# A copy of q placed above the relative terms in SBUF, and a pair of low-rank products split in two

## The chip, the cores and the metric

The kernel runs on one NeuronCore of a Trainium2 chip. The metric is the device time of one execution in microseconds (us). Before the change three runs gave a median of 3314.61 us (3313.37 to 3317.38).

## The reference

Two attention layers work on one image of 48 x 48 positions with 768 channels. Each adds its result to its input:

```python
x = x + L0(_gn(x))          # plus low-rank terms on q and v
x = x + L1(_gn(x))

# inside a layer, per head (12 heads of 64):
qkv  = x @ qkv_w + qkv_b
attn = einsum('bqc,bkc->bqk', q * scale, k)
rel_h = einsum('bhwc,hkc->bhwk', r_q, Rh)      # by the query's row
rel_w = einsum('bhwc,wkc->bhwk', r_q, Rw)      # by the query's column
attn = softmax(attn + rel_h[..., :, None] + rel_w[..., None, :])
out  = (attn @ v) @ proj_w + proj_b
```

`_gn` is a group norm over 32 groups of 24 channels. In layer 0 a product of rank 16 (`FacTu_w`, `q_facts_w`, `v_facts_w`, `FacTv_w`) is added to q and v; the kernel folds it into the weights.

## The kernel before

All data is 32-bit. Channels lie on partitions. The 2304 positions are cut into six blocks of 384 for the projections (`b`), and into four blocks of 512 and one of 256 for attention's queries. Twelve heads are six pairs, and a "half" is three pairs.

A layer runs in this order.

1. **Norm** (`group_norm`, from L194). Channel means and variances are summed over groups by small matmuls (`sum_mean`, then `sum_var`) and spread back over channels by others (`bc_mean`, then `bc_rstd`). The order of PE's instructions is held by `in_order`. While one step waits for DVE, PE is given other work: `next(between)` resumes the generator `low_rank` (L313 to L339), which in layer 0 forms the low-rank products `psl` (L336) and copies them to SBUF (`low`, L339). In its loop over two halves each resume issues two products. In layer 1 there is no low-rank term and the generator is empty.
2. **k and v** (`project_kv`). Results are stored to scratch memory in HBM. The last tile of values, `v_2_2`, is stored by 16 DMAs of GpSimd's queue (L599).
3. **q** (`project_q`, from L601). For each half, six blocks are multiplied (L695) and biased (L701), stored as two parts, high and low (`store`, L628), and copied by ACT to the tile `columns` with rows and columns of the image exchanged (L711). PE then forms `rel_h` from each block (L635, stored at L661). When the half is complete, `rel_w` is formed from `columns` (L635 again, sixteen steps), split into a high part by ACT (L389) and a low part by DVE (L390), and stored by two DMAs of 2592 KB each on GpSimd's queue (L684).
4. **Attention** (`attend_plain`). For each pair and query block, eighteen key tiles are multiplied into score tiles `ps_sc` (eight matmuls on q and k, then two on the relative terms `rel`, L951). ACT takes the exponential into an SBUF tile `pt` (L978), DVE adds up the sums (L984), and PE multiplies `pt` with the values (`ps_ov`) nine key tiles later. There are three PSUM buffers for scores and nineteen `pt` buffers. The next block's queries and relative terms are loaded on SP's queue, in program order: two loads of q (L929), then 24 of rel (L939, L943). They go to one of two buffer sets in turn, `in0` and `in1`.
5. **Output** (`out_project`), whose weights `wproj` are loaded during attention (L1247).

**SBUF.** Pools are stacked. A pool that opens where another has closed reuses its addresses, and the first writer of a new tile waits for every access to the tiles that lay there (`reuse_waits`). Within a pool with one buffer per tag, tags are laid out in the order in which they are first allocated. The q stage has the pools `p1_one` (`columns` and the two `relw` parts, 27 KB per partition each) and then `p1_b` (blocks of q and their parts). When they close, attention's pools start at the same address: `p3_w` (output weights and their sums, 31.5 KB), `in1` (22 KB), `t` (8 KB: `rec`, `o`), `h` (10 KB: `sum` and its parts), `p` (nineteen `pt` of 4 KB), `kv` and `in0`. Before them, the k and v stage had its own pools at that address.

Block 0 of attention reads its queries from `in0`, block 1 from `in1`. The pairs of half 0 come first, so block 0 uses the `relw` stored for half 0; the tiles of half 1 are stored last before attention.

Of the kernel before, what the change touches and what calls it, by code (L numbers as in the profile page):

```python
# [18 lines left out]
P = 128  # L19
# [4 lines left out]
HG = 48  # L24
N = HG * HG
# [4 lines left out]
HP = CT // 2  # L30
# [41 lines left out]
def compute(ctx: ExitStack, tc: tile.TileContext, x, layers, out, run, bad):  # L72
# [45 lines left out]
    if shifted:  # L118
        parts = [
            (HG, [[0, HG], [-1, HG]], (HG, HG)),  # L120
            (KG, [[0, NG], [-1, KG], [0, HG]], (NG, KG, HG)),
        ]
        hot = scratch("hot", [HG + KG, N])
    else:
        parts = [
            (KG, [[-8, 2], [-1, 8], [0, KG]], (2, 8, KG)),
            (KG, [[0, 2], [0, 8], [-1, KG]], (2, 8, KG)),
        ]
# [65 lines left out]
    def group_norm(xT, raw, gn, between, beside):  # L194

        root = gn.tile([GH, 1], F32, tag="root", name="root")
        in_order(nc.scalar.activation(root, eps, AF.Sqrt))  # L200
        with tc.tile_pool(name="ps_gn", bufs=1, space=PSUM) as ps_gn:
            mv = gn.tile([P, CT, nc.vector.BN_AGGR_DIM], F32, tag="mv", name="mv")
            for t in range(CT):
                nc.vector.bn_aggr(mv[:, t, :], stats[:, t, :, :].rearrange("p b s -> p (b s)"))

            def over_group(values, tag):

                ps = ps_gn.tile([GH, 2], F32, tag="sum", name=f"sum_{tag}")
                for t in range(HP):
                    in_order(nc.tensor.matmul(  # L210
                        ps, lhsT=gin[:, t, :], rhs=values[:, :, t],
                        start=(t == 0), stop=(t == HP - 1),
                    ))
                mean = gn.tile([GH, 2], F32, tag=f"g_{tag}", name=f"g_{tag}")
                in_order(nc.vector.tensor_scalar(mean, ps, 1.0 / GSZ, None, ALU.mult))
                next(beside, None)
                return mean

            def to_channels(values, tag):
                ps = ps_gn.tile([P, 2, HP], F32, tag="bc", name=f"bc_{tag}")  # L220
                for t in range(HP):
                    in_order(nc.tensor.matmul(
                        ps[:, :, t], lhsT=gout[:, ts(t, P)], rhs=values, start=True, stop=True
                    ))
                c = gn.tile([P, CT], F32, tag=f"c_{tag}", name=f"c_{tag}")
                in_order(nc.vector.tensor_copy(c, ps.rearrange("p i t -> p (i t)")))
                return c

            def halves(values):
                return values.rearrange("p (i t) -> p i t", i=2)  # L230

            next(between, None)
            mean = to_channels(over_group(halves(mv[:, :, 0]), "mean"), "mean")
            next(between, None)
            var = gn.tile([P, CT], F32, tag="var", name="var")
            nc.vector.tensor_sub(var, mv[:, :, 0], mean)
            nc.vector.tensor_mul(var, var, var)
            in_order(nc.vector.tensor_add(var, var, mv[:, :, 1]))
            next(beside, None)
            rstd = over_group(halves(var), "var")  # L240
            nc.scalar.activation(rstd, rstd, AF.Sqrt, bias=eps)
            in_order(nc.vector.reciprocal(rstd, rstd))
            next(beside, None)
            rstd = to_channels(rstd, "rstd")

        def normalise(b):
            for t in range(CT):
                nc.vector.tensor_scalar(  # L248
                    xT[b][:, t, :], raw[b][:, t, :], mean[:, t : t + 1],
                    rstd[:, t : t + 1], ALU.subtract, ALU.mult,  # L250
                )

        return normalise

    class Weights:
# [5 lines left out]
        PARTS = {"k": (1, 2 * P), "q": (0, HP * P)}  # L261
# [51 lines left out]
        def low_rank(self, room):  # L313


            if self.ly.lora is None:
                return
            fuT = room.tile([RANK, C], F32, tag="x", name="fuT")
            for r in range(1, 4):
                nc.gpsimd.tensor_copy(  # L320
                    self.facts[:, :, r * 32 : r * 32 + RANK], self.facts[:, :, 0:RANK]
                )
            for half in range(2):
                cols = ts(half, HP * P)
                ps = self.ps.tile([P, HP * P], F32, tag="f", name=f"psu_{half}")
                for t in range(HP):
                    in_order(nc.tensor.transpose(
                        ps[0:RANK, ts(t, P)], self.fu[:, half * HP + t, :], ident
                    ))
                nc.vector.tensor_copy(fuT[:, cols], ps[0:RANK])  # L330
            for half in range(2):
                yield
                cols = ts(half, HP * P)
                for i in range(2):
                    ps = self.ps.tile([P, HP * P], F32, tag="f", name=f"psl_{half}_{i}")
                    in_order(nc.tensor.matmul(  # L336
                        ps, lhsT=self.facts[:, i, :], rhs=fuT[:, cols], start=True, stop=True
                    ))
                    nc.scalar.copy(self.low[:, i, cols], ps)  # L339
# [261 lines left out]
    def project_q(ly, li, xT, weights, qd, rel_d):  # L601

        PARTS = range(1 if shifted else 2)
        PART = F32 if shifted else F32R
        lines = HG // NQB
        with ExitStack() as es:
            one = es.enter_context(tc.tile_pool(name="p1_one", bufs=1, **REUSE))
# [52 lines left out]
                for found, part in zip(rel_d[0][half], parts):  # L660
                    nc.gpsimd.dma_start(found[:, :, ts(b, QB)], part.bitcast(F32))  # L661

            def rel_w(half, x, between):

                parts = [
                    one.tile([P, HP, N], PART, tag=f"rel{i}", name=f"relw_{half}_{i}")[0 : 2 * HG]
                    for i in PARTS
                ]
                for l0 in range(0, HG, 3):
                    if l0 == HG // 2:  # L670
                        between()
                    ps = ps_rel.tile(
                        [2 * HG, 3, HP, HG], F32, tag="rel", name=f"psc_{half}_{l0}"
                    )
                    positions(1, ps, lambda l: x[:, :, l, :], l0, 3)
                    to = [
                        r.rearrange("p t (h w) -> p w t h", w=HG)[:, l0 : l0 + 3] for r in parts
                    ]
                    if shifted:
                        nc.scalar.copy(to[0], ps)  # L680
                    else:
                        in_parts(*to, ps)
                for found, part in zip(rel_d[1][half], parts):
                    nc.gpsimd.dma_start(found, part.bitcast(F32))  # L684

            for half in range(2):
                w, _ = weights.take("q", half)
                columns = one.tile([P, HP, HG, HG], F32, tag="columns", name=f"columns_{half}")
                for b in range(NQB):
                    x = bp.tile([P, HP, QB], F32, tag="x", name=f"x_q_{half}_{b}")  # L690
                    for pr in range(HP):
                        pair = half * HP + pr
                        ps = ps_mm.tile([P, QB], F32, tag="mm", name=f"ps_q_{pair}_{b}")
                        for t in range(CT):
                            nc.tensor.matmul(  # L695
                                ps, lhsT=w[:, t, ts(pr, P)], rhs=xT[b][:, t, :],
                                start=(t == 0), stop=(t == CT - 1),
                            )
                        while later:
                            later.pop()()  # L700
                        nc.vector.tensor_scalar(  # L701
                            x[:, pr], ps, weights.bt[:, pair : pair + 1], ly.q_scale,
                            ALU.add, ALU.mult,
                        )
                    def keep():
                        store(qd[half], b, x, f"xs_q_{half}_{b}", HD**-0.5)


                    if b < NQB - 1:
                        keep()  # L710
                    nc.scalar.copy(  # L711
                        columns[:, :, :, b * lines : (b + 1) * lines],
                        x.rearrange("p t (h w) -> p t w h", w=HG),
                    )
                    later.append(lambda b=b, x=x: rel_h(half, b, x))
                    if half == 0 and b == HB:
                        weights.fold(weights.take("q", 1)[0], 0, 1, ps_mm)
                while later:
                    later.pop()()
                rel_w(half, columns, keep)  # L720


    recs = None if shifted else [scratch(f"rec{li}", [NH, N]) for li in range(2)]
# [619 lines left out]
```

## Time and profile before

The profiled execution took 3314.17 us, of which 3312.4 us is the span that the profile covers.

| engine | busy us | share of the span |
|---|---|---|
| PE (matmul) | 3218.9 | 97% |
| PE (weight load, overlapped) | 2016.1 | 61% |
| DVE | 2098.9 | 63% |
| ACT | 1446.3 | 44% |
| GpSimd | 373.8 | 11% |

| line | what | count | mean us |
|---|---|---|---|
| L951 | score matmul on q and k | 8640 | 0.371 |
| L951 | value matmul | 4320 | 0.551 |
| L978 | exponential | 1080 | 0.941 |
| L711 | copy to `columns` | 24 | 2.185 (median) |
| L684 | store of a `relw` part, issue to landing | 8 | 18.4 (median; 14.8 to 25.2) |

The rows of a timeline give the start in us from the span's beginning, the time taken by the merged instructions, the engine, the line, the operation, the tiles written and read, the count, and in brackets how long the engine had been idle and what ended that. SPq and POOLq are the queues in which SP and GpSimd issue DMAs. PEclk, or the granted clock, is the share of full speed that the TensorE clock had.

Layer 0 runs to about 1546 us (its attention begins at 503), layer 1's attention begins at 2125.

### The profile page before, as it was taken

To read this page: it belongs to the slowest core of one execution; us is meant where nothing else is said; L and a number is where in the kernel's file an instruction comes from. 1 tells how busy PE (TensorE), PEld (TensorE's weight loads), DVE (VectorE), ACT (ScalarE), POOL (GpSimd) and SP (SyncE) were. 2 spreads that over 40 slices of the span, in tenths; PEclk is the share of its full clock that TensorE was granted. 3 is DMA by queue.
4 is the path that set the end of the run, shared out by engine and by line. 5 is a ranking of instruction groups with operands and counts; after the bars stand their busy time and mean duration, and the time that the engine had idled before them with its cause. 6 is when DMAs were issued, how large, how long until landed. Compare 5 with 4: busy or idle time off the path is not lost.

```text
span 3312.4 us, 50021 instructions
## 1 busy us (share of the span) xinstructions
PE 3218.9 (97%) x19708; PEld 2016.1 (61%) x19708; DVE 2098.9 (63%) x2275; ACT 1446.3 (44%) x1655; POOL 373.8 (11%) x701
## 2 busy tenths in 40 slices
PE   8999997999999999999989999699999999999998
PEld 5556665666656565665555566466666565656665
DVE  8432445777777777777775234377777777777764
ACT  3101344555556555553011024355656565655511
POOL 2144110000000000000012531100000000000000
PEclk9999998999999999999999999899999999999999
DMA  7333486272625262634234345753535262534251
GB/s 263 129 84 84 132 256 179 62 153 67 150 64 153 63 151 65 142 71 157 100 124 144 57 116 196 239 122 98 119 86 130 77 137 76 134 83 123 58 193 59
DMA packets 219092, 405.61 MB, mean 122 GB/s; under 512 B 41393, under 2 KB 108881, under 8 KB 215009
## 3 DMA queue, kind: packets, MB, share of 16 engines
q1 hardware_dynamic: 177984, 260.08, 31.5%
q0 software_dynamic: 40864, 142.23, 13.7%
q8 instruction: 159, 2.61, 0.3%
q14 instruction: 85, 0.69, 0.1%
HBM read 253.27 MB, written 148.89 MB: 121 GB/s over the span
## 4 chain that ended last, share of the span: by engine, by line
PE 83%; issue 10%; POOL 2%; DMA 2%; DVE 1%; SPq 1%; ACT 0%; POOLq 0%; DVEq 0%; ACTq 0%
PE ps_sc L951 34%; PE ps_ov L951 25%; PE ps_v L521 7%; PE psy L1170 7%; PE ps_k L521 4%; PE ps_q L695 2%; PE ps_d L951 1%; DMA f_r<-relw 1%; POOL f_q L628 1%; POOL f_r L661 1%; POOL f_k L565 1%; PE psr L635 0%; PE psn L1197 0%; DMA flat<-in_relh_t_dram 0%; ACT pt L978 0%
## 5 line engine op out<-in xcount | busy, mean ns | idle before, releaser
L984 DVE TENSOR_TENSOR sum<-sum,pt 128x1024 f32<-128x1024 f32 (+1 forms) x960 | 1071.0, 1116 | 188.5 <-ACT pt L978 98.2
L951 PE MATMUL ps_sc<-q,k 64*128 64x512 f32 (+1 forms) x8640 | 1087.0, 371 | 45.5 <-ACT pt L978 44.2
L978 ACT ACTIVATE pt<-ps_sc 128x1024 f32<-128x1024 f32 (+1 forms) x1080 | 1011.1, 941 | 191.7 <-PE ps_sc L951 106.1
L951 PEld LDWEIGHTS ps_sc<-q,k 64*128 64x128 f32 x8640 | 788.0, 186 | 250.2 <-ACT pt L978 48.1
L951 PE MATMUL ps_ov<-pt,v 128*64 128x512 f32 (+1 forms) x4320 | 857.7, 551 | 0.0
L951 PEld LDWEIGHTS ps_ov<-pt,v 128*64 128x64 f32 x4320 | 301.2, 137 | 497.5 <-issue 443.0
L951 PE MATMUL ps_sc<-rel,places 64*128 64x512 f32 (+1 forms) x2160 | 411.5, 371 | 0.0
L695 PE MATMUL ps_q<-xT,w_q 128*128 128x384 f32 x864 | 285.1, 489 | 0.6 <-DVE v L585 0.6
L1029 POOL DMA_DIRECT2D f_rec<-rec x120 | 58.3, 490 | 1819.3 <-DVE rec L1018 1819.1
L1023 ACT ACTIVATE o<-o,v_bias 128x512 f32<-128x512 f32 (+1 forms) x60 | 40.9, 682 | 449.8 <-DVE o L1022 449.8
L695 PEld LDWEIGHTS ps_q<-xT,w_q 128*128 128x128 f32 x864 | 163.3, 191 | 109.8 <-issue 2.3
L951 PEld LDWEIGHTS ps_sc<-rel,places 64*128 64x128 f32 x2160 | 210.8, 185 | 28.5
L1018 DVE RECIPROCAL rec<-ps_d 128x512 f32<-128x512 f32 (+1 forms) x60 | 181.8, 3031 | 2.5 <-PE ps_d L951 2.5
L984 DVE TENSOR_TENSOR sum<-pt 128x1024 f32<-128x1024 f32 (+1 forms) x60 | 67.1, 1119 | 182.5 <-ACT pt L978 182.5
L599 POOL DMA_DIRECT2D f_v<-v x288 | 137.3, 485 | 106.1 <-DVE v L585 94.7
L521 PE MATMUL ps_k<-xt,w_k 128*128 128x384 f32 x432 | 143.4, 488 | 3.5 <-DVE xt L425 2.6
L701 DVE TENSOR_SCALAR x_q<-ps_q,bt 128x384 f32<-128x384 f32 x72 | 44.2, 617 | 159.1 <-PE ps_q L695 159.1
L993 ACT CAST sum<-sum 128x1024 bf16<-128x1024 f32 (+1 forms) x60 | 57.6, 960 | 165.2 <-DVE sum L984 165.2
L521 PEld LDWEIGHTS ps_k<-xt,w_k 128*128 128x128 f32 x432 | 81.6, 190 | 62.9 <-PE ps_k L521 3.0
L521 PE MATMUL ps_k<-xT,w_k 128*128 128x384 f32 x324 | 114.8, 508 | 4.7 <-DVE xT L248 4.6
L996 DVE TENSOR_TENSOR sum<-sum,sum 128x1024 bf16<-128x1024 f32 (+1 forms) x60 | 67.2, 1119 | 61.5 <-ACT sum L995 61.5
L994 DVE TENSOR_TENSOR sum<-sum,sum 128x1024 f32<-128x1024 f32 (+1 forms) x60 | 67.2, 1119 | 61.5 <-ACT sum L993 61.5
(172 smaller groups left out, 2384.5 us busy)
## 6 DMA issues: line engine op xcount, KB each, us to landing
rel<-f_r SPq DMA_DIRECT2D x1152, 96.0 KB, 4.3
f_k<-xs POOLq DMA_DIRECT2D x72, 384.0 KB, 2.9
f_q<-xs_q POOLq DMA_DIRECT2D x48, 576.0 KB, 3.8
k<-f_k SPq DMA_DIRECT2D x48, 576.0 KB, 4.7
q<-f_q SPq DMA_DIRECT2D x96, 256.0 KB, 3.2
f_r<-relh POOLq DMA_DIRECT2D x48, 432.0 KB, 5.0
f_r<-relw POOLq DMA_DIRECT2D x8, 2592.0 KB, 18.4
f_v<-v POOLq DMA_DIRECT2D x288, 48.0 KB, 2.0
```

The lines of the kernel that those rows point to most:

```text
L521: nc.tensor.matmul(ps, lhsT=x, rhs=y, start=(t == 0), stop=(t == HP - 1))
L599: nc.gpsimd.dma_start(vd[to : to + KG, :], v[ts(r, KG), k])
L695: nc.tensor.matmul(ps, lhsT=w[:, t, ts(pr, P)], rhs=xT[b][:, t, :], start=(t == 0), stop=(t == CT - 1),)
L951: in_order(nc.tensor.matmul(*args, **kwargs))
L978: nc.scalar.activation(pt, ps[:, :, 0 : self.n], AF.Exp)
L984: nc.vector.tensor_add(self.sum, self.first if kt == 1 else self.sum, pt)
L993: nc.scalar.copy(hi, self.sum)
L994: nc.vector.tensor_sub(self.sum, self.sum, hi)
L996: nc.vector.tensor_sub(lo, self.sum, mid)
L1018: nc.vector.reciprocal(self.rec, ps)
L1029: nc.gpsimd.dma_start(recs[li][2 * self.pair + r : 2 * self.pair + r + 1, to], self.rec[r * HD : r * HD + 1, :],)
L1170: nc.tensor.matmul(ps, lhsT=w[left_of][:, t, ts(co, P)], rhs=right[right_of][:, t, :], start=(t == 0), stop=(t == HP - 1),)
```

## The change

Two parts. In `low_rank`, the second half's two products are no longer issued by one resume: the generator yields once more, between them. `group_norm` resumes it a third time, behind the `sum_var` matmuls and ahead of the square root. In `project_q`, the two `relw` tiles of a half are allocated at the start of the half, before `columns`, and handed to `rel_w`; what is computed and the order in which it is issued stay the same. On the engines' queues only layer 0's norm changes order: on PE the second product of the second half stands behind the three `sum_var` matmuls, on ACT the square root stands ahead of the copy of that product.

```diff
@@ group_norm
             rstd = over_group(halves(var), "var")
+            next(between, None)
             nc.scalar.activation(rstd, rstd, AF.Sqrt, bias=eps)
@@ low_rank
             for half in range(2):
-                yield
                 cols = ts(half, HP * P)
                 for i in range(2):
+                    if half == 1 or i == 0:
+                        yield
                     ps = self.ps.tile([P, HP * P], F32, tag="f", name=f"psl_{half}_{i}")
@@ project_q
-            def rel_w(half, x, between):
-
-                parts = [
-                    one.tile([P, HP, N], PART, tag=f"rel{i}", name=f"relw_{half}_{i}")[0 : 2 * HG]
-                    for i in PARTS
-                ]
+            def rel_w(half, x, parts, between):
+
                 for l0 in range(0, HG, 3):
...
             for half in range(2):
                 w, _ = weights.take("q", half)
+
+                relw = [
+                    one.tile([P, HP, N], PART, tag=f"rel{i}", name=f"relw_{half}_{i}")[0 : 2 * HG]
+                    for i in PARTS
+                ]
                 columns = one.tile([P, HP, HG, HG], F32, tag="columns", name=f"columns_{half}")
...
-                rel_w(half, columns, keep)
+                rel_w(half, columns, relw, keep)
```

## The prediction

> **What bounds it.** Read first was the page's busy table: PE is busy 97% of the span, so only PE idle time, or PE time at a low clock, is left to win. Next came the list of waits, for a wait of PE that is long and rare:
>
> ```profile
> ACT L978 <- DMA f_r<-relw: 45.9, 2, 23.0
> ...
> PE ps_sc L951 <- ACT pt L978: 44.2, 2, 22.5
> ```
>
> Columns: who waited for whom, us in total, times, longest. Twice in the span, once per layer, PE stands still for about 22 us because the exponential of L978 stands still for about 23 us, and that waits for a store of the `relw` tiles to memory. The timeline shows the place in layer 0 (weight loads left out):
>
> ```profile
> 504.32 0.53 POOL L684 DMA_DIRECT2D f_r<-relw  x1 [5.87 <-ACT relw L389]
> ...
> 505.37 0.52 POOL L684 DMA_DIRECT2D f_r<-relw  x1 [0.53 <-DVE relw L390]
> ...
> 506.41 0.40 PE L951 MATMUL ps_sc<-rel,places 64*128 64x512 f32 x2
> 519.17 2.43 SPq L929 DMA_DIRECT2D q<-f_q  x2
> ...
> 526.90 1.28 ACT L978 ACT_TABLE_LOAD   x1 [22.88 <-DMA f_r<-relw]
> ...
> 528.19 2.85 ACT L978 ACTIVATE pt<-ps_sc 128x1024 f32<-128x1024 f32 x3
> 529.27 2.07 PE L951 MATMUL ps_sc<-q,k 64*128 64x512 f32 x8 [22.46 <-ACT pt L978]
> ```
>
> Three score tiles are ready at 506.81 and fill all three PSUM buffers; the first exponential then waits for both stores of half 1's `relw`. Block 0 of attention does not read them: it needs half 0, whose stores were issued at 408. So this is a wait for memory to come free, not for data. Layer 1 is alike (PE from 2130.15 to 2151.84). The windows view adds the granted clock (third number from the right) and the DMA rate (last):
>
> ```profile
> 506.90:510.00 3.10, 0.00 (x0) 0.00 (x0) 0.00 (x0) 0.00 (x0) 0.00 (x0) 1.00 1.04 285
> 510.00:514.00 4.00, 0.00 (x0) 0.00 (x0) 0.00 (x0) 0.00 (x0) 0.00 (x0) 0.62 0.94 325
> ...
> 525.00:527.00 2.00, 0.00 (x0) 0.00 (x0) 0.00 (x0) 0.10 (x1) 0.00 (x0) 0.50 0.31 100
> ...
> 530.00:535.00 5.00, 5.00 (x28) 3.85 (x26) 3.68 (x3) 3.10 (x4) 0.00 (x0) 0.51 1.10 156
> 535.00:540.00 5.00, 5.00 (x46) 4.41 (x44) 4.34 (x4) 3.98 (x4) 0.00 (x0) 1.00 1.12 159
> ```
>
> PE goes on at half clock until about 535: the pause costs more than its length.
>
> **Part 1, the tiles' order in memory.** From the tile sizes, in KB per partition above the pools' base: each `relw` part and `columns` take 27 (3 x 48 x 48 floats). Before, `columns` lies at 0-27, the high part at 27-54, the low part at 54-81. Attention starts from the same base: output weights and their sums 0-31.5, the second query set 31.5-53.5, two small pools to 71.5, then the `pt` buffers. The first `pt`, at 71.5-75.5, and the first `sum`, at 61.5, fall on the low part and inherit its store; the second query set falls on the high part. After: high part 0-27, low part 27-54, `columns` 54-81. The first `pt` and `sum` fall on `columns`, whose last reader is a PE matmul of L635 done before attention's first score. The built program says the same: the first exponential no longer names either store; all engines' orders are unchanged but for part 2.
>
> *What goes.* (a) PE's idle time: 529.27 - 506.81 = 22.46 us, and 2151.84 - 2130.15 = 21.69. What is late next? The exponential's table load, 1.28 us, now waits for the first score, done at 504.4, so the first exponential runs 505.7-506.7 and frees a PSUM buffer just before PE asks at 506.81: next to no wait. The other seventeen `pt` of the block wait for query and `relh` stores issued by 497.73 or earlier, and for old weight loads. Total 44.15. (b) The slow clock: score tiles 3 to 5 take 529.27 to 535.40 = 6.13 us, tiles 6 to 8 3.47, so 2.66 is lost; layer 1's same 15 tiles need 19.54 us against 20.23 (chain of waits), so 1.97. Here the Trainium skill ("TensorE: Matmul & The Clock Gate", Part 1) would put less: half rate for about 3.4 us after a pause, 1.7 us lost per layer, 3.4 in all. The rows show 5.9 us at half clock and 4.63 lost; I take the rows. Gross: 48.78.
>
> *What comes.* (c) The second query set now lies on the low part, so block 1's loads on SP's queue (two q, then 24 rel, with all later loads queued behind them) wait for the second store, not the first: 519.17 becomes the landing of the low part, seen at 526.9. Who waits for them: PE, at block 1. PE gets there at 506.81 + 17.57 (15 tiles: 20.23 - 2.66) + 7.87 (first batch of values) = 532.25 and needs rel 0 at 533.2, after the first eight score matmuls. How long do loads take to reach that? Block 2's show it: q at 549.07, the eighth rel at 553.20, 96 KB landing 4.3 us after issue (median), so 8.4. From 526.9 that is 535.3, 2.1 late; in layer 1 2149.3 + 8.4 = 2157.7 against 2156.5, 1.2 late: 3.3 in all. On the other side, the low part should land sooner, since today block 1's loads run beside it from 519.2. The skill ("DMA: Bandwidth & Descriptors", Queues, rings and completion order) has each DMA engine take turns among its queues packet by packet; 4.5 of the stores' 5.3 MB had moved by 519.2 at about 300 GB/s, the remaining 0.8 MB would need 2.7 us and land about 522: cost 0. But the rate is 100 GB/s and DMA share 0.31 in the last 2 us, which looks like a few late engines, not competition. Between 0 and 3.3 I take 1.5.
>
> (d) `columns` is now first written over the last value tile `v`, so that copy (L711, on ACT, ahead of the `relh` casts that PE's ps_rel buffers wait for) waits for its 16 stores. In layer 0 the last is issued at 306.3 and lands 2.0 to 3.2 us later, by 309.5; the copy runs at 312.54. Cover: 3 us. Layer 1 already has this wait today and its copy starts at 1942.26, right behind the activation before it: 0. Without the cover a late store would cost its lateness, once per layer. (e) `relw`'s first writes and the output-weight load (now behind the high part's store) come long after what they wait for; the load is issued at 562.50: 0. Half 1's tiles, allocated earlier, are still first written where they were, by ACT and DVE, after half 0's readers: 0.
>
> **Part 2, the split products (layer 0 only; layer 1 has no low-rank term).** The timeline around the norm:
>
> ```profile
> 30.75 2.90 PE L336 MATMUL psl<-fuT,facts 16*128 16x384 f32 x4
> ...
> 31.52 0.17 DVE L238 TENSOR_TENSOR var<-var,mv 128x6 f32<-128x6 f32 x1
> ...
> 33.58 0.32 PE L210 MATMUL sum_var<-var,gin 128*16 128x2 f32 x6
> ...
> 34.77 1.41 PE L222 MATMUL bc_rstd<-g_var,gout 16*128 16x2 f32 x6 [0.87 <-DVE g_var L242]
> ```
>
> Two products of 1.45 us each stand ahead of `sum_var`, whose input is ready at 31.69. With one moved behind, `sum_var` starts at about 32.15. Its answer would be back 1.19 later, plus 0.2 because the first product's copy holds ACT until 32.89: 33.55. But the moved product fills PE from 32.47 to 33.92, so `bc_rstd` starts at 33.95: 0.8 gained, not 1.4. On ACT the square root now stands ahead of the last copy, as it must. Lower end 0, if the k stage behind waits for DVE or stores anyway; upper 1.4. I take 0.8.
>
> **Sum**, against the profiled run's own 3314.17 (span 3312.4 plus 1.8 around it; the median, 3314.61, is 0.4 above): 44.15 + 4.63 - 1.5 + 0.8 = 48.1 less, **3266.1**, so 3266. Everything behind each gap is PE-bound and moves up with it.
>
> **Rivals.**
> *Late block-1 loads (13%).* The stores slow down beside running score matmuls. For: half 0's stores ran beside a busy PE and took up to 25.2 us, not 21.5. Against: k and q traffic shared the queues then. From 505.37 that lands at 530.6, rel 0 at 539.0, 5.8 late; layer 1 4.9 late. That is longer than the 4.2 us after which the clock fell in the trace (the mean 0.62 of 510-514 puts it at 511.0), and the skill's clock page speaks against such pauses too: it puts the drop after about 3.4. So the 4.63 of (b) would be paid again: 44.15 + 4.63 - 10.7 - 4.63 + 0.8 = 34.2, **3280**.
> *No release (5%).* The first exponential named several semaphores and the profile names only the last; if another, unseen, is as late, nothing moves: **3314**. Against: the program's waits, read above, leave only PE and ACT.
> *Slower (4%).* The same loads of (c), further: PE's pause would only move from block 0 to the start of block 1 and grow there. The 4.63 of (b) is then not won, so what must be eaten is 44.15 + 0.8 = 45.0 over two layers, 22.5 in each. That is so when the second store lands at 533.2 + 22.5 - 8.4 = 547.3, some 42 us after its issue: from there on the change loses, 10 us for each further 5. At 47 us PE waits 27.6 and 26.7, together 54.3, and the time is 3314.2 - 45.0 + 54.3 = **3323**. For it: only that the store now overlaps attention. Against: no `relw` store took over 25.2.
>
> **Numbers.** Forecast 78%, late loads 13%, no release 5%, slower 4%. About 0.2% (6.6 us) is what can be told from no change here: faster 0.92, same 0.04, slower 0.04. Range: no stall and 1.4 from part 2 gives 3264, less 2 for the scatter between runs; upward to the late loads' 3280 and 1 more: 3262 to 3281.
>
> **What would show it.** The two longest waits above gone; the table load near 504.4 and the fourth score tile near 506.8 at full clock; block 1's q issued between 522 and 527 instead of 519.17, with at most 2 us of PE idle at its first rel; `columns`' first copy where it is; `bc_rstd` near 33.95. Wrong if PE stands still at 506.8 again, or longer than 4 us near 532.

## The result and the profile after

The changed kernel took 3269.30 us (median of four runs, 3265.58 to 3271.80) beside 3314.95 us for the kernel before (four runs, 3313.37 to 3317.38). The ratio is 0.9861, with a 95% interval of 0.9844 to 0.9878: about 46 us or 1.4% faster. The forecast was 3266, in a range of 3262 to 3281. The profiled execution after is a rather slow one: 3271.64 us, of which the span is 3269.8. Lines of the changed kernel have moved: the scores are L954, the exponential L981, the `relw` stores L682, the q loads L932, the rel loads L942 and L946, `psl` L338, `ps_k` L523, the output projection L1173.

The waits of PE and ACT for a `relw` store are gone from the list of waits. The timeline of layer 0 at attention's start, from the kernel after (weight loads and DVE left out):

```profile
504.57 1.28 ACT L981 ACT_TABLE_LOAD   x1 [0.44 <-PE ps_sc L954]
...
505.86 19.65 ACT L981 ACTIVATE pt<-ps_sc 128x1024 f32<-128x1024 f32 x18
...
506.94 1.21 PE L954 MATMUL ps_sc<-q,k 64*128 64x512 f32 x8
...
527.42 0.81 SPq L932 DMA_DIRECT2D q<-f_q  x2
...
532.25 1.21 PE L954 MATMUL ps_sc<-q,k 64*128 64x512 f32 x8
...
535.08 0.47 PE L954 MATMUL ps_sc<-rel,places 64*128 64x512 f32 x1 [1.62 <-DMA rel<-f_r]
...
536.36 0.76 PE L954 MATMUL ps_sc<-rel,places 64*128 64x512 f32 x1 [0.80 <-DMA rel<-f_r]
536.36 2.47 PE L954 MATMUL ps_sc<-q,k 64*128 64x512 f32 x8
```

The table load now names PE's first score and not a store, all eighteen exponentials run in one go, and the fourth score tile follows the third without a pause. Block 1 begins at 532.25 where it began at 557.30: 25.05 us won. Then some of it is paid back: the q loads wait for the low part until 527.42, PE stands 1.62 and 0.80 us at block 1's first relative terms, and behind that eight score matmuls take 2.47 us in place of 1.21. The windows view of four stretches of the same kernel (columns: stretch, length, busy of PE, weight loads, DVE, ACT, GpSimd, granted clock, DMA share, GB/s) shows why:

```profile
503.00:532.29 29.29, 29.26 (x219) 19.24 (x218) 23.57 (x20) 21.56 (x22) 1.05 (x2) 1.00 0.70 215
532.29:535.70 3.41, 1.64 (x11) 0.81 (x9) 1.60 (x2) 1.05 (x1) 0.00 (x0) 1.00 1.09 173
535.70:542.53 6.83, 6.17 (x30) 5.34 (x32) 1.23 (x1) 3.07 (x3) 0.00 (x0) 0.50 1.03 182
542.53:545.94 3.41, 3.41 (x32) 3.13 (x30) 2.78 (x3) 2.47 (x3) 0.00 (x0) 1.00 0.99 244
```

Block 0 runs through at full clock. Behind it PE stands still for 2.42 us in two pieces, and from 535.70 to 542.53 its clock is at half. Block 1's first batch (nine key tiles' scores and the values behind them) takes from 532.25 to 557.30, 25.05 us, where before it took 19.05: 6.0 us are given back in layer 0. Layer 1 has the same shape, with a pause of 0.46 us and without the loss of clock:

```profile
2129.24 0.81 SPq L932 DMA_DIRECT2D q<-f_q  x2
...
2137.51 0.49 PE L954 MATMUL ps_sc<-rel,places 64*128 64x512 f32 x1 [0.46 <-DMA rel<-f_r]
```

The norm of layer 0, with the split products (timeline of the kernel after):

```profile
30.26 1.37 PE L338 MATMUL psl<-fuT,facts 16*128 16x384 f32 x2
31.56 0.32 PE L210 MATMUL sum_var<-var,gin 128*16 128x2 f32 x6
31.81 1.64 PE L338 MATMUL psl<-fuT,facts 16*128 16x384 f32 x2
33.26 1.27 PE L222 MATMUL bc_rstd<-g_var,gout 16*128 16x2 f32 x6
35.30 8.77 PE L523 MATMUL ps_k<-xT,w_k 128*128 128x384 f32 x18 [0.77 <-DVE xT L249]
```

and the first products of k in the kernel before:

```profile
36.95 7.55 PE L521 MATMUL ps_k<-xT,w_k 128*128 128x384 f32 x18 [0.77 <-DVE xT L248]
```

The products of k start 1.65 us earlier (0.49 of that lies ahead of the split: `psl` itself began earlier). But the eighteen of them take 8.77 us instead of 7.55, so that at their end 0.43 us is left, and the q stage starts at 299.10, against 298.91 before.

### The profile page after: what moved, and what is told of

Read it like the earlier page. It is cut to its first block, busy times and chain, and to the rows that moved or that the text cites. A ratio compares the mean times of both kernels' runs of the same rounds, so it can differ in the third digit from the quotient of the medians.

```text
span 3269.8 us, 50021 instructions
## 1 busy us (share of the span) xinstructions
PE 3219.1 (98%) x19708; PEld 2010.7 (61%) x19708; DVE 2098.2 (64%) x2275; ACT 1446.6 (44%) x1655; POOL 374.0 (11%) x701
## 4 chain that ended last, share of the span: by engine, by line
PE 88%; issue 6%; DVE 2%; DMA 1%; POOL 1%; SPq 1%; ACT 1%; POOLq 0%; DVEq 0%
PE ps_sc L954 34%; PE ps_ov L954 25%; PE ps_v L523 7%; PE psy L1173 7%; PE ps_q L698 6%; PE ps_k L523 4%; PE ps_d L954 1%; PE psr L637 1%; DMA f_r<-relw 1%; POOL f_k L567 1%; PE psc L637 0%; DVE relw L392 0%; PE psn L1200 0%; ACT relw L391 0%; DMA flat<-in_relh_t_dram 0%
## 5 line engine op out<-in xcount | busy, mean ns | idle before, releaser
L981 ACT ACTIVATE pt<-ps_sc 128x1024 f32<-128x1024 f32 (+1 forms) x1080 | 1011.2, 941 | 192.1 <-PE ps_sc L954 105.8
L954 PE MATMUL ps_sc<-q,k 64*128 64x512 f32 (+1 forms) x8640 | 1086.1, 371 | 1.3 <-DVE relw L392 0.6
L954 PEld LDWEIGHTS ps_sc<-q,k 64*128 64x128 f32 x8640 | 786.6, 186 | 208.1 <-issue 43.9
L954 PE MATMUL ps_ov<-pt,v 128*64 128x512 f32 (+1 forms) x4320 | 857.7, 551 | 0.0
L954 PEld LDWEIGHTS ps_ov<-pt,v 128*64 128x64 f32 x4320 | 301.1, 137 | 497.6 <-issue 443.0
L954 PE MATMUL ps_sc<-rel,places 64*128 64x512 f32 (+1 forms) x2160 | 415.3, 371 | 2.9 <-DMA rel<-f_r 2.9
L954 PEld LDWEIGHTS ps_sc<-rel,places 64*128 64x128 f32 x2160 | 213.3, 185 | 33.2 <-DMA rel<-f_r 2.9
L523 PE MATMUL ps_k<-xt,w_k 128*128 128x384 f32 x432 | 143.4, 488 | 3.5 <-DVE xt L427 2.6
L523 PE MATMUL ps_k<-xT,w_k 128*128 128x384 f32 x324 | 116.4, 513 | 4.7 <-DVE xT L249 4.6
L523 PEld LDWEIGHTS ps_k<-xt,w_k 128*128 128x128 f32 x432 | 81.6, 190 | 62.9 <-PE ps_k L523 3.0
```

Of the source, the lines that this page charges most:

```text
L523: nc.tensor.matmul(ps, lhsT=x, rhs=y, start=(t == 0), stop=(t == HP - 1))
L954: in_order(nc.tensor.matmul(*args, **kwargs))
L981: nc.scalar.activation(pt, ps[:, :, 0 : self.n], AF.Exp)
```

## The experiments

Two theories were set against each other for the gain: that the first exponential's memory is free, so that PE no longer stands still; and that something else in part 1 does it, the early allocation of the `relw` tiles or the place of the query set. For what was given back: that block 1's loads are held by the wait for their memory; or that the DMA engines are full and they could land no earlier. All ratios are to the kernel before on the same chip, with 95% intervals.

**One part at a time.** `e1_place_only` has the new order of tiles and the old loop in `low_rank`; `e2_split_only` has the split and the old order.

```diff
 e1: group_norm, low_rank
             rstd = over_group(halves(var), "var")
-            next(between, None)
...
             for half in range(2):
+                yield
                 for i in range(2):
-                    if half == 1 or i == 0:
-                        yield
```

> Part 1 alone: the relw tiles below columns, the low-rank products as before. Theory (the first exponential was held by the store of the tile whose memory its pt takes): the whole gain, 3266 to 3272, the two waits of 22 us gone, bc_rstd again near 34.8 us. Rival (the split products carry a share of the 45 us): slower than the full change by 1.5 us or more, near 3271 to 3273 throughout.

> Part 2 alone: columns at the bottom as before, the second product behind sum_var. Theory: bc_rstd near 33.3 us as in the full change, but the time within 1.5 us of before (3313 to 3316), since at the second block of k only 0.4 us of the lead was left; both waits of about 22 us stay. Rival (the lead of 1.65 us at the first k matmul survives): 3313 or less, 1.6 us under before in every round's comparison.

Part 1 alone: 3271.79 us, ratio 0.9864 (0.9849 to 0.9880). Part 2 alone: 3313.62 us, ratio 0.9993 (0.9985 to 1.0001), not told from no change; its table load is where it was before:

```profile
527.38 1.28 ACT L980 ACT_TABLE_LOAD   x1 [22.91 <-DMA f_r<-relw]
```

Part 1 has all of the gain that can be told from noise. Part 2 is not shown to be nothing: the interval leaves room for up to 5 us, and ten of the 17 runs of the kernel before on that chip lie above all 13 of `e2`.

**Which tile's place matters.** The edits of `e4` and `e5` are given in short form. `e4_columns_mid` keeps the early allocation but puts `columns` between the parts: the query set of block 1 then lies on `columns`, the first `pt` still on the low part.

```diff
 e4: project_q, order of allocation
-                relw = [ high, low ]
-                columns = ...
+                high
+                columns = ...
+                low
```

> The full change with columns between the parts: high part at the bottom, columns at 27 to 54 KB, low part on top. The first pt and sum lie on the low part again, the second query set lies on columns. Theory: the first exponential waits for the second store again; block 1's loads no longer wait for a store but for the last reader of columns, so they are issued near 503 us and share the DMA engines with the stores, whose landing moves from 527 to between 527 and 534 us: time 3314 to 3330, PE idle 22 to 29 us per layer. Rival (the gain came from where the second query set lies, or from the tiles' being allocated early): 3266 to 3275.

Measured: 3317.48 us, ratio 1.0004 (0.9997 to 1.0011). The timeline of this kernel:

```profile
503.37 0.81 SPq L934 DMA_DIRECT2D q<-f_q  x2
...
529.66 1.28 ACT L983 ACT_TABLE_LOAD   x1 [25.36 <-DMA f_r<-relw]
532.03 2.08 PE L956 MATMUL ps_sc<-q,k 64*128 64x512 f32 x8 [24.90 <-ACT pt L983]
```

Block 1's loads are issued 16 us earlier than before, and nothing is gained; PE waits 2.4 us longer, and the store lands later too. So neither the early allocation nor the query set's place by itself makes the gain.

`e5_high_on_top` gives half a dose: `columns` at the bottom, the low part above it, the high part on top, so that the first `pt` waits for the earlier of the two stores.

```diff
 e5: project_q, order of allocation
-                relw = [ high, low ]
-                columns = ...
+                columns = ...
+                relw = [ low, high ], handed on in the old order
```

> Dose: columns at the bottom as before, but the parts exchanged, low part at 27 to 54 KB and high part on top, with the split products. The first pt lies on the high part, stored first. Theory (the wait is as long as the store that lies beneath): the exponential starts when the first store lands, near 519.5 us instead of 526.9, PE idle about 14.5 us per layer instead of 22; block 1's loads wait for the second store and come in time (needed near 545): 7.5 us less per layer, 3298 to 3301. Rival (any wait for a store costs the same, or both stores land together without block 1's loads beside them): 3309 to 3315.

Measured: 3297.04 us, ratio 0.9949 (0.9932 to 0.9965). Its timeline:

```profile
518.85 1.28 ACT L981 ACT_TABLE_LOAD   x1 [15.09 <-DMA f_r<-relw]
521.22 2.08 PE L954 MATMUL ps_sc<-q,k 64*128 64x512 f32 x8 [14.60 <-ACT pt L981]
```

PE's pause follows the landing of the store that lies under the first `pt`: 22.5 us with the second store, 14.6 with the first, none with neither. The time was a little below what was expected; in layer 0 the clock was back 3.1 us after PE went on (524.34), where the kernel before took 5.6 (534.89), which saves about 1.2 us; layer 1 gave some 0.4 of that back (5.1 us against 4.4).

**What is given back in block 1.** `e3_low_below` lets the query set wait for the first store and not for the second: low part at the bottom, high part above it, `columns` on top. `e6_low_below_no_split` is the same without part 2.

```diff
 e3: project_q
                 relw = [
                     one.tile(..., tag=f"rel{i}", ...)
-                    for i in PARTS
-                ]
+                    for i in reversed(PARTS)
+                ][::-1]
```

> The full change with the two relw parts exchanged: low part at the bottom, high part above it, columns on top, so that the second query set lies on the part that is stored first. Theory (what block 1 lost, 2.4 us of PE idle and some 3.5 us at half clock in layer 0 and about 1 us in layer 1, came from its loads waiting for the second store): loads issued near 519.5 us, no PE pause near 533, no half clock there, time 3263 to 3266 and all runs within 2 us of each other. Rival (the loads then run beside the tail of the stores and come no earlier): 3266 to 3272 as in the full change, rel 0 landing near 535 again.

> As the run with the low part at the bottom, but with the low-rank products as before: what the split is worth once block 1 has no pause. Theory (the split's lead is eaten in the k stage): within 1 us of that run. Rival: 1.6 us slower than it.

> The full change once more, beside the others. Its four runs so far were 3265.6, 3267.0, 3271.6, 3271.8. Theory (PE's short pause at block 1 sometimes drops the clock to half for some 6 us and sometimes not): again two clusters some 5 us apart, the slower ones at clock 0.993. Rival (plain scatter): one cluster around 3269.

`e3_low_below` took 3267.47 us (0.9856, 0.9841 to 0.9871), `e6_low_below_no_split` 3269.15 (0.9863, 0.9847 to 0.9880), and the whole change once more 3269.70 (0.9864, 0.9849 to 0.9879): not told apart by their intervals. With the split the medians are 2.1 us lower (`after_again` against `e1_place_only`) and 1.7 lower (`e3_low_below` against `e6_low_below_no_split`, on two chips); that is what the two rivals had (1.5 or more, and 1.6), but neither difference is clear of the scatter. The two clusters that were expected of `after_again` did not show in its four runs (3269.08 to 3272.11). The timeline of `e3_low_below`:

```profile
517.68 3.71 SPq L932 DMA_DIRECT2D q<-f_q  x2
...
532.70 0.47 PE L954 MATMUL ps_sc<-rel,places 64*128 64x512 f32 x1 [1.16 <-DMA rel<-f_r]
534.21 0.47 PE L954 MATMUL ps_sc<-rel,places 64*128 64x512 f32 x1 [1.04 <-DMA rel<-f_r]
```

PE still waits 2.2 us for the loads. Counted from each execution's first `ps_q`, they are issued after 220.6 us here and after 228.3 to 228.4 in three executions of the whole change, but rel 0 reaches PE after 235.6 here and after 235.5 to 236.0 there: nearly eight microseconds of lead gained nothing. Issued beside the stores' tail, the loads took that much longer. Here the second theory was right, as far as it concerns loads issued this late.

To give them a still earlier start, `e8_loads_free` puts the whole of what block 1 needs first on `columns`.

```diff
 e8: attend_plain, on top of e3
-            in1, tp, hp, pp, kv, in0 = pools("in1", "t", "h", "p", "kv", "in0")
+            tp, in1, hp, pp, kv, in0 = pools("t", "in1", "h", "p", "kv", "in0")
+            in1.tile([P, 640], F32, tag="pad", ...)
...
 fetch_queries: rel tiles allocated from the last to the first, then q
```

> Low part at the bottom, high part above it, columns on top as in e3_low_below; in attention's memory the small pool t stands ahead of in1, in1 is laid out with its relative terms from the last to the first and its q behind them, and 2.5 KB of it are left empty, so that block 1's two q and the first of its three rel tiles lie on columns as the first pt and sum do. Nothing is left out of the computation. The loads of q and rel 0 then wait for no store of relw, only rel 1 and rel 2 do, for the high part. If block 1's loads are late because they wait for the memory of a part (step c of the prediction), they are issued near 505 to 510, PE does not stand still at block 1's first rel and its clock does not drop there: 3.3 us of idle time over both layers and up to 3 us of half clock are won against e3 and the changed kernel, 3264 (3262 to 3267). Rival: the queues' engines are full with the two stores, so that the loads issued beside them land when the stores do and slow them; then PE's pause of about 2 us stays, at the same rel or at rel 1, and the time stays at 3267 to 3270.

> The kernel of e3_low_below once more, on the same chip as e8_loads_free, to compare the two. All theories: 3266 to 3269, PE idle about 2 us at block 1's first rel tiles.

Measured: 3292.66 us, ratio 0.9925 (0.9911 to 0.9938), 26 us slower than `e3_again` beside it with 3266.53 (0.9847, 0.9834 to 0.9861). Neither theory had this. The loads were issued at 504.69, PE's pause in layer 0 shrank to 1.02 us, and the clock stayed up. What cost the time is elsewhere. In the list of waits of this kernel:

```profile
PE ps_sc L955 <- DMA rel<-f_r: 6.6, 4, 3.1
PE psy L1174 <- DMA xT<-f_o: 6.4, 1, 6.4
PE psy L1174 <- DMA oT<-f_o: 6.2, 1, 6.2
```

In layer 1 PE waits 5.6 us for relative terms, and both output projections start late. The last load of the first projection's input was issued at 1522.48, right as the last value matmul ended (1522.44), as a load does whose tile lies on memory that this matmul reads. So the same kind of wait had been made at the other end of attention. That the 2.5 KB left empty had pushed the tiles there is the reading of it; the next run, in which they are not left empty, no longer has this wait.

`e9_loads_free_same_size` takes that out: the three bf16 parts of `sum` lie ahead of `in1` in place of the empty space, and the pools together are as large as before.

```diff
 e9: attend_plain, on top of e8
-            tp, in1, hp, pp, kv, in0 = pools("t", "in1", "h", "p", "kv", "in0")
-            in1.tile([P, 640], F32, tag="pad", ...)
+            tp, h3, in1, hp, pp, kv, in0 = pools("t", "h3", "in1", "h", "p", "kv", "in0")
...
-                            hp.tile([P, 2, QS], BF16, tag=f"sum{i}", ...)
+                            h3.tile([P, 2, QS], BF16, tag=f"sum{i}", ...)
```

> As e8_loads_free, but the 2.5 KB are not left empty: the three bf16 parts of sum (6 KB) lie ahead of in1 instead, so that all pools together are as large as in the changed kernel and the end of attention and the output projections find the memory that they find there. Nothing is left out of the computation. Theory from e8: its 26 us were the waits of both output projections (6.4 and 6.2 us and the clock after them) and a late block 1 in layer 1, not block 1's loads in layer 0; here the first projection wait goes, layer 0's pause at block 1 is about 1 us at full clock, and the time is 3264 to 3268, or some 5 us more if layer 1's late q is due to the order of the loads and not to the 2.5 KB. Rival: loads issued beside the stores slow both, in both layers, and it stays at 3280 or above.

> The whole change once more, on the same chip as e9_loads_free_same_size, to compare the two. All theories: 3267 to 3272, about 2 us of PE idle at block 1's first rel tiles, with or without half clock behind it.

Measured: 3285.87 us, ratio 0.9921 (0.9907 to 0.9934), beside the whole change with 3269.06 (0.9864, 0.9849 to 0.9879). The rival's number (3280 or above) came, though not in layer 0. There the theory held: block 1 runs without any pause. The windows view of 531 to 545 us, first `e9_loads_free_same_size`, then the whole change (`after_again`):

```profile
531.00:545.00 14.00, 14.00 (x110) 9.49 (x108) 10.26 (x9) 11.17 (x11) 0.00 (x0) 1.00 0.90 185
```

```profile
531.00:545.00 14.00, 12.00 (x96) 9.35 (x94) 8.68 (x8) 9.27 (x10) 0.00 (x0) 1.00 0.95 204
```

PE is busy for all of the 14 us in the first; it lacks 2.0 in the second. But the total is 17 us worse. Against `after_third`, from profile to profile (18.1 us between the spans): layer 0 from its first `ps_q` to its first projection 2.9 shorter, layer 1's like stretch 3.3 longer, and 8.6 and 7.7 longer behind the two attentions; the start of q differed by 1.5. Most of the last two is one more wait of the same kind (4.84 us of PE here, 5.03 in layer 1), with half clock behind it:

```profile
1533.56 5.83 PE L1173 MATMUL psy<-oT_t,wproj_s 128*128 128x384 f32 x12 [4.84 <-DVE oT_t L427]
```

With `t` moved to the front, the projection's tile `oT_t` falls on `o` and `rec`. Its first write comes at 1532.14, after their last store has landed (1531.67); in the changed kernel (`after_third`) it comes at 1526.32, with that store still under way until 1532.92. In layer 1, PE also waits 2.19 us for the relative terms of block 0: with the first query set laid out in the new order too, their loads are issued up to 2112, beside the stores, and not by 2090.

`e10_all_free` keeps the gain and takes these two away.

```diff
 e10: attend_plain, on top of e3
-            in1, tp, hp, pp, kv, in0 = pools("in1", "t", "h", "p", "kv", "in0")
+            in1a, h3, tp, in1, hp, pp, kv, in0 = pools(
+                "in1a", "h3", "t", "in1", "h", "p", "kv", "in0")
...
 fetch_queries, second query set only: rel 2 and rel 1 from in1a, rel 0 and then q from in1
 the three bf16 parts of sum from h3
```

> On top of e3_low_below, with all pools together as large as there: rel 2 and rel 1 of the second query set in a pool of their own at the front, then the three parts of sum, then t, then rel 0 and q of the second set, then sum and the pt buffers. Block 1's q and rel 0 lie on columns as in e9_loads_free_same_size, but t no longer lies under the projection's oT_t, and the first query set keeps its layout, so that block 0's loads in layer 1 are issued as early as in the changed kernel. Nothing is left out of the computation. Theory: what e9 lost behind attention and in layer 1 goes (8.6, 7.7 and 3.3 us), what it won in layer 0 stays (2.9 us against the change with its clock kept), and perhaps 0.5 us in layer 1: 3266 (3264 to 3268), ratio 0.985, no PE pause in block 1 and full clock there. Rival: another tile inherits a late store (kept_p and kept_u lie on t and wait for its last stores), and it is 3270 or above.

Measured: 3263.67 us (3263.45 to 3265.50 in five runs), ratio 0.9847 (0.9834 to 0.9861). In the list of PE's waits no relative terms and no output projection are left. The timeline and the windows view of this kernel:

```profile
501.11 0.81 SPq L942 DMA_DIRECT2D q<-f_q  x2
...
503.40 0.52 POOL L682 DMA_DIRECT2D f_r<-relw  x1 [0.52 <-DVE relw L392]
```

```profile
531.00:545.00 14.00, 14.00 (x110) 9.36 (x108) 11.67 (x9) 9.93 (x10) 0.00 (x0) 1.00 1.09 179
```

q is issued ahead of both stores (the first is issued at 502.35), and PE is busy throughout block 1. So what block 1 gave back can be won when its first loads are issued ahead of both stores, and for that their tiles must not lie on the stores' memory: `e9` and `e10` both have it, about 2.9 us in layer 0 against the changed kernel with its clock kept. Whether the whole time is better is less sure. All five runs lie below all twelve of the changed kernel (3265.58 to 3272.11) and its median is 5 us lower, but these ran on other chips. The intervals of the two ratios (to 0.9861 here, from 0.9844 there) still meet, and `e3_again`, with a pause in block 1, has the same ratio of 0.9847.

**The clock.** The profiled executions side by side. The stretch is layer 0 from its first `ps_q` to its first output projection; the clock is that of 531 to 545 us. "Most idle in one step" is explained below the table.

| kernel | pauses in block 1, us | most idle in one step, us | clock | stretch, us |
|---|---|---|---|---|
| before | (22.46 in block 0) | | 0.86 | 1247.5 |
| after | 1.62 + 0.80 | 1.77 | 0.76 | 1228.3 |
| e1_place_only | 1.45 + 0.77 | 1.49 | 0.76 | 1228.2 |
| e3_again | 1.13 + 1.21 | 1.90 | 0.88 | 1226.8 |
| e6_low_below_no_split | 0.93 + 1.00 | 1.47 | 0.88 | 1226.2 |
| e3_low_below | 1.16 + 1.04 | 1.16 | 1.00 | 1225.4 |
| after_third | 1.45 + 0.74 | 1.45 | 1.00 | 1225.3 |
| after_again | 1.02 + 0.98 | 1.09 | 1.00 | 1225.1 |
| e9_loads_free_same_size | none | 0 | 1.00 | 1222.4 |
| e10_all_free | none | 0 | 1.00 | 1222.3 |

Three executions of the same program, the whole change, are among them: two kept the clock and one lost it, for 3.1 us. Without any pause it is about 2.9 us less again.

What differs between them is in the traces. In each of the fourteen, all changes of the granted clock lie whole multiples of 3.413 us apart (to within 0.005 us): in the kernel after at 361.62, 535.70 and 542.53, for one, which are 51 steps and 2. Against the kernel these steps lie elsewhere in each execution. The third column cuts the pauses by these steps and gives the longest idle time that one of them has. In the kernel after, one step (532.29 to 535.70, shown above) has the first pause whole and a part of the second, and the clock falls at its end. In `after_again` a border falls between the two pauses:

```profile
530.90:534.32 3.42, 2.33 (x13) 0.86 (x9) 2.31 (x2) 1.05 (x1) 0.00 (x0) 1.00 1.04 212
534.32:537.73 3.41, 2.50 (x22) 2.36 (x24) 0.00 (x1) 1.80 (x2) 0.00 (x0) 1.00 1.02 218
```

Idle for 1.09 and 0.91 us, neither step lost the clock. In this block every execution with 1.47 us or more in one step lost it, and every one with 1.45 or less kept it. That is no rule: in layer 1 of `e8_loads_free` a step with 1.63 us idle (2128.79 to 2132.20) left the clock at 1.00.

## Why the prediction was right, point by point

The mechanism was right, and the two misses of size are in what comes in place of the old wait. The profiled execution lies 5.5 us above the forecast: 1.4 of it is the mis-sized term (c), some 3 the clock behind it, and the rest is of the size of part 2 and the scatter.

- **The bound, and that the wait is for memory: right.** `e4` and `e5` show it: the pause follows whichever store lies under the first `pt`, and `e4` has the early allocation and a free place for the query set without any gain.
- **(a) and (b), 48.78 us won: right.** Together 49.3 were won. (The stretch at half clock, read as 5.9 us, was 5.6.) Block 1 was put at 532.25 and began at 532.25 in layer 0. The table load came at 504.57 (504.4), the fourth score tile at 506.94 (506.8), at full clock. In layer 1 block 1's start moved from 2179.25 to 2135.61, of which 19.39 had been won before that layer's attention; the 24.25 left are 23.66 by the prediction.
- **(c), block 1's loads: the mechanism right, the size wrong.** The q loads came at 527.42, just past the stretch named, and rel 0 at 535.08, where the upper bound had 535.3. PE stood 2.42 and 0.46 us, together 2.88: near the upper end of 3.3, not the 1.5 taken, and more in layer 0 than the 2 us named as the sign. The second store did not land sooner when the loads no longer ran beside it (527.4 against 526.8), so the argument for the lower end failed. This mis-sized term is 1.4 us of the error.
- **The clock in (c): not priced.** The prediction let the clock fall only after a pause of 4.2 us, and used that in the rival of late loads alone. Pauses of 1.9 to 2.4 us in two pieces lost it in some executions, for up to 3.1 us. The trace of the kernel before had a sign of that in its layer 1, where the clock fell 2.2 us after PE had stopped, not 4.2:

```profile
2130.15:2132.33 2.18, 0.00 (x0) 0.00 (x0) 0.00 (x0) 0.00 (x0) 0.00 (x0) 1.00 0.78 228
2132.33:2136.00 3.67, 0.00 (x0) 0.00 (x0) 0.00 (x0) 0.00 (x0) 0.00 (x0) 0.50 0.95 336
```

- **(d) and (e), nothing: right.** `columns`' first copy runs at 312.73, right behind the activation ahead of it.
- **Part 2, 0.8 us: right in its place; what is left of it at the end is open.** From the start of `psl` to the first `ps_k` the norm takes 5.04 us against 6.20. But PE runs at half clock there, and the clock comes back between 38.1 and 42.3 us, differently in each profiled execution, so that the first eighteen `ps_k` took from 7.53 to 9.04 us. The q stage starts at 297.1 to 300.4 in the eleven profiled executions with the split and at 298.9 to 300.7 in the three without: a gain of 0.8 us can't be seen in that. `e2` puts the whole at -1.5 to +0.1 thousandths, or 5 us less to 0.3 more, which holds both nothing and the forecast; its median, like the two other pairs with and without the split, is about 2 us on the side of a gain.

Put together: 3314.17 - 44.15 - 4.63 + 2.9 gives 3268.3 with the clock kept, and 3271.4 with it lost. The three medians of the whole change are 3269.1 to 3269.7, and its profiled execution, with the clock lost, took 3271.64. None of the rivals happened: the loads were late by 2.4 us and not 5.8, the first exponential was released, and the changed kernel's second store landed 22 us after its issue.

## What to carry to other kernels

When an engine waits for a transfer whose data it doesn't read, ask what lay at its output's address before: changing the order of allocation can put a tile that is long done under the first tile of the next stage, at no cost in work. Go through all the tiles of both stages when doing so, since the pending store still lies under something: here the next block's loads inherited it, two attempts to free those as well made the same wait at the far end of the stage and were some 20 and 17 us slower than the change, and the third, with these tiles placed by what lay under them, freed them at no such cost. And be slow to count a microsecond gained while the clock is at half speed: here the clock's return differed by 4 us between executions.

## What the runs showed of the hardware

- Half clock followed pauses of about 2 us in two pieces in some executions and not in others of the same program (table above); the length of the pauses doesn't decide it (2.19 us kept the clock, 1.93 lost part of it), but how they fall on the steps of 3.413 us between which the granted clock changed goes with it in the seven executions with pauses in that table. The Trainium skill ("TensorE: Matmul & The Clock Gate", Part 1) puts the drop after a whole idle window of about 3.4 us, by which nothing would be lost here; the measurement differs, since steps with 1.47 to 1.90 us idle were followed by half clock. It also has the windows run free of the kernel, and with that the traces agree: in three executions of the whole change the clock first falls at 30.53, 29.15 and 29.67 us, and the other changes follow in whole steps from there.
- After a long pause, the return to full clock took 3.1 us of work in layer 0 and 5.1 in layer 1 of `e5`, and 5.6 and 4.4 in the kernel before. In the kernel after the clock was at half for 6.8 us.
- Loads issued beside the second of two large stores gained nothing by an early issue. Issued 220.6 and 228.3 us after the first `ps_q` (`e3_low_below` and the kernel after), block 1's first relative terms reached PE at 235.6 and 236.0, and the early q issue itself took 3.71 us where it took 0.81 behind the stores. With q issued ahead of both stores (`e10`, 501.11 against 502.35 and 503.40) they came in time, as far as PE shows; `e8`, with q at 504.69 and the first store at 504.05, still left a pause of 1.02 us.
